# Second attention: four heads to a step, the router with its weights held, and another order of what fills the steps

## The chip, the core and the metric

One core of a Trainium2 chip runs the whole program. TensorE (PE; its weight loads are PEld) multiplies matrices, VectorE (DVE), ScalarE (ACT) and GpSimd (POOL) do the rest, SyncE (SP) issues most transfers. The metric is the device time of one execution in microseconds (us); for the kernel before, the median of three runs. The clock of TensorE can be granted in part; the profile states the granted share as PEclk.

## The reference, cut to what matters

Four sequences of 512 tokens with 512 channels in float32 go through an attention, a feed-forward net with ternary weights, a state-space scan, and a last block of a second attention and a mixture of experts. The change lies in the last block (batch and rows as the kernel has them: 4 x 512):

```python
h = x + attention(rmsnorm(x, ln1_w), ...)      # 16 heads of 32, causal, softmax over 512 keys
out = h + moe(rmsnorm(h, ln2_w), ...)
# moe: a shared expert for all tokens, and the best two of seven routed ones
shared = expert_ffn(x, sh_gate, sh_up, sh_down)
logits = x @ router_w + router_b               # 512 -> 7
probs = sigmoid(logits); scores, idx = top_k(probs, 2)
# expert_ffn: h = silu(x @ wg) * (x @ wu) / 8;  return h @ wd
```

## The kernel before

Inputs stay in SBUF as `xs[b]`, four tiles of 128 tokens x 4 x 512 channels. The stages run one after the other: first attention, ternary net, scan, second attention, experts. The framework that the kernel is written in places the semaphores and orders the instructions of DVE, ACT, POOL and the queues by itself; where `manual_schedule` names PE, PE's instructions keep the order of the code.

**PSUM** in the second attention is cut into two pairs of banks (`pair`, each 2 x 512 floats a partition) and four single banks (`bank`).

**The first attention** (`scores` in `attend`, L318 to L329) computes four heads at a time: 32 rows of channels for each head, so the four matmuls stand on four row quarters of the array and write to two pairs.

**The second attention** works on `pairs`, 128 steps: batch b, group g of four heads, row tile t of 128 queries, and a pair p of heads. A step runs, in this order, `soften` of its own pair (scores into one pair of banks; the mask added on DVE, the maximum on DVE, the exponentials and their sums on ACT), `turn` of the pair two steps back (the probabilities transposed on PE, copied out by DVE for the first head and ACT for the second), every second step `weigh` of a finished row tile (probabilities times values, four heads on four column quarters), and after the last row tile of a group `divide` and `turn_back`. Widths grow with t: 128, 256, 384, 512 columns.

Three generators give a step more work, one piece per `next`:

- `enter(b)`, the way in: layer norm and RMS norm (DVE, ACT, POOL), transposes, the two latents (L715), and for each row tile values, queries, keys and rotation (L734 to L764; the projection holds a pair of banks, `pqd`), then transposes. The first batch's runs before the loop; the next one's begins at step 9 of 32, one piece a step.
- `leave(b)`, the way out: output projection (L984), residual and its write to `acc`, RMS norm, transposes, the write of `hrows`, and the router (L1010: for each row tile the tokens are the weights of the matmul and the 7 columns of `wr` move). It begins at step 6 of the next batch.
- `shared(b)`, the shared expert: transposes, gate and up (L943, one pair of banks `pge` for each half of the inner width, used by gate in one piece and by up in the next), Silu on ACT (L948), down (L957), added to `xs[b]` (L961).

After the loop come the last batch's way out, with `shared(0)` between its output projection and its norm, then the head of the experts' stage, where `shared(1)` and `shared(2)` stand between the small steps of the routing, then 38 tiles of routed tokens, then `shared(3)`, and at the end each of 16 tiles of `acc` is read (L1396), added to `xs` (L1397) and written out (L1398).

Of the kernel before, what the change touches and what calls it, by code (L numbers as in the profile page):

```python
# [45 lines left out]
def block_kernel(ctx: ExitStack, tc: tile.TileContext, a: dict, out: bass.AP):  # L46
# [16 lines left out]
    def pair(name):  # L63
        return banks["pair"].tile([P, 2, 512], F32, tag="pair", name=name)

    def bank(name):
        return banks["bank"].tile([P, 512], F32, tag="bank", name=name)
# [703 lines left out]
    with tc.tile_pool(name="c_f", bufs=2, reuse_waits="tile") as cf, tc.tile_pool(  # L771
# [31 lines left out]
        def turn(b, n, half):  # L803
            bu = [bank("bu") for _ in range(2)]
            for i in range(2):
                k = 2 * half + i
                for t in range(NT):
                    nc.tensor.transpose(  # L808
                        bu[i][:, t * P : (t + 1) * P], scaled[b, n][t][:, k * P : (k + 1) * P], ident
                    )  # L810
            turned[b, n, half] = bu
# [9 lines left out]
        def weigh(b, n, half):  # L821
            if half == 0:
                cb = c1.tile([P, T], F32, tag="cb", name="cb", bufs=3)
                nc.sync.dma_start(cb, c_rows[b, n].partition_broadcast(P))
                weighed[b, n] = cb
            hc = c2.tile([P, 2, T], F32, tag="hc", name="hc", bufs=3)
            nc.gpsimd.tensor_tensor(  # L827
                hc, states.pop((b, n, half)), weighed[b, n].unsqueeze(1).to_broadcast([P, 2, T]), ALU.mult
            )
            states[b, n, half] = hc  # L830
# [93 lines left out]
    def fetch_shared():  # L924

        for tag, name, shape in (
            ("w_a", "sh_gate", [P, NK, INTER]), ("w_b", "sh_up", [P, NK, INTER]), ("w_c", "sh_down", [P, NI, C])
        ):
            sh[name] = dw.tile(shape, F32, tag=tag, name=name)
            nc.sync.dma_start(sh[name], by_rows(a[name]))  # L930
# [35 lines left out]
    with tc.tile_pool(name="d_1", bufs=1) as d1, tc.tile_pool(name="d_2", bufs=2) as d2, tc.tile_pool(  # L966
# [9 lines left out]
        def leave(b, oT):  # L976


            h = hs[b]
            ss = d2.tile([P, NT], F32, tag="ss", name="ss")  # L980
            for t in range(NT):
                y = bank("y")
                for k in range(NK):
                    nc.tensor.matmul(  # L984
                        y, oT[:, k, t * P : (t + 1) * P], wow[:, k, :], start=k == 0, stop=k == NK - 1
                    )
                nc.vector.tensor_tensor(h[:, t, :], h[:, t, :], y, ALU.add)
                n = b * NT + t
                nc.sync.dma_start(acc[n * P : (n + 1) * P, :], h[:, t, :])
                sq = d2.tile([P, C], F32, tag="row", name="sq")  # L990
                nc.scalar.activation(sq, h[:, t, :], AF.Square, accum_out=ss[:, t : t + 1])
                if t == NT - 1:
                    rs = root_inverse(d2, ss, RMS_EPS, 1.0 / C, "rms")
                yield
            hT = far.tile([P, NK, T], F32, tag="hT", name="hTr")
            for t in range(NT + 1):
                if t < NT:
                    nc.vector.scalar_tensor_tensor(
                        h[:, t, :], h[:, t, :], rs[:, t : t + 1], ln2, ALU.mult, ALU.mult
                    )  # L1000
                if t > 0:
                    transpose_into(hT, h[:, t - 1, :], (t - 1) * P)
                if t < NT:
                    yield
            nc.sync.dma_start(by_tokens(hrows, b), h)
            yield
            for t in range(NT):
                pl = bank("plr")
                for k in range(NK):
                    nc.tensor.matmul(  # L1010
                        pl[:, :NR], hT[:, k, t * P : (t + 1) * P], wr[:, k, :],
                        start=k == 0, stop=k == NK - 1,
                    )
                nc.vector.tensor_tensor(logit[:, b * NT + t, :], pl[:, :NR], br, ALU.add)
                if t % 2 == 1:
                    yield

        pairs = [
            (b, g, t, p) for b in range(B) for g in range(NG) for t in range(NT) for p in range(HG // 2)
        ]
        probs, turned_probs, sums, averages, rows, outs = {}, {}, {}, {}, {}, {}

        def soften(b, g, t, p):
            w = (t + 1) * P
            qkT = ready[b][0]
            if (b, g) not in sums:
                sums[b, g] = d2.tile([P, NT, HG], F32, tag="sums", name="sums")  # L1030
            sc = pair("scd")
            for i in range(2):
                at = slice((2 * p + i) * D, (2 * p + i + 1) * D)
                nc.tensor.matmul(  # L1034
                    sc[:, i, :w], qkT[at, g, t * P : w], qkT[at, NG + g, :w], start=True, stop=True
                )
            nc.vector.tensor_tensor(  # L1037
                sc[:, :, t * P : w], sc[:, :, t * P : w],
                neg.unsqueeze(1).to_broadcast([P, 2, P]), ALU.add,
            )  # L1040
            nm = d3.tile([P, 2], F32, tag="nm", name="nm")
            nc.vector.tensor_reduce(nm, sc[:, :, :w], AX.X, ALU.max, negate=True)  # L1042
            pr = d3.tile([P, 2, T], F32, tag="pr", name="pr")
            for i in range(2):
                nc.scalar.activation(  # L1045
                    pr[:, i, :w], sc[:, i, :w], AF.Exp, bias=nm[:, i : i + 1],
                    accum_out=sums[b, g][:, t, 2 * p + i : 2 * p + i + 1],
                )
            probs[b, g, t, p] = pr

        def turn(b, g, t, p):
            w = (t + 1) * P
            pr = probs.pop((b, g, t, p))
            for i in range(2):
                tp = bank("tpd")
                for j in range(t + 1):
                    nc.tensor.transpose(  # L1057
                        tp[:, j * P : (j + 1) * P], pr[:, i, j * P : (j + 1) * P], ident
                    )
                pt = d3.tile([P, T], F32, tag="pt", name="ptd", bufs=7)  # L1060
                if i == 0:
                    nc.vector.tensor_copy(pt[:, :w], tp[:, :w])  # L1062
                else:
                    nc.scalar.copy(pt[:, :w], tp[:, :w])
                turned_probs[b, g, t, 2 * p + i] = pt

        def weigh(b, g, t):
            if t == 0:
# [29 lines left out]
        def turn_back(b, g):  # L1098
            if g == 0:
                outs[b] = d1.tile([P, NK, T], F32, tag="oT", name="oTd")  # L1100
            o = rows.pop((b, g))
            tp = bank("tpb")
            for t in range(NT):
                nc.tensor.transpose(tp[:, t * P : (t + 1) * P], o[:, t, :], ident)
            nc.scalar.copy(outs[b][:, g, :], tp)

        with tc.manual_schedule(engines={mybir.EngineType.PE}):
            for _ in come:
                pass
            left = iter(())  # L1110
            n = len(pairs)
            each = n // B
            for m in range(n + 9):
                b, at = divmod(m, each)
                if m < n:
                    soften(*pairs[m])
                if 2 <= m < n + 2:
                    turn(*pairs[m - 2])
                if m >= 4 and m % 2 == 0 and m - 3 < n:
                    weigh(*pairs[m - 3][:3])  # L1120
                if m >= 6 and m - 6 < n and pairs[m - 6][2:] == (NT - 1, 0):
                    divide(*pairs[m - 6][:2])
                if m >= 8 and m - 8 < n and pairs[m - 8][2:] == (NT - 1, 0):
                    turn_back(*pairs[m - 8][:2])

                if m == (B - 1) * each:
                    fetch_shared()
                if m >= each and at == 6:
                    left = leave(b - 1, outs[b - 1])
                if at >= 7:  # L1130
                    next(left, None)
                if at == 9:
                    come = enter(b + 1, d2) if b + 1 < B else iter(())
                if at >= 9:
                    next(come, None)

            for _ in range(2):
                next(left)
            for _ in shared(0, d1, "lat"):
                pass  # L1140
            for _ in left:
                pass
# [4 lines left out]
    with tc.tile_pool(name="e_1", bufs=1, reuse_waits="tile") as e1, tc.tile_pool(  # L1147
# [7 lines left out]
            nc.sync.dma_start(wgu[:, e, :, INTER:], by_rows(a["r_up"][e]))  # L1155
            nc.sync.dma_start(wdn[:, e], by_rows(a["r_down"][e]))

        second, third = shared(1, e1, "hid"), shared(2, e1, "hid")

        def go(parts, n):  # L1160
            for _ in range(n):
# [226 lines left out]
                turn_hidden(i)  # L1388


        for _ in shared(3, e1, "hid"):
            pass
        for b in range(B):
            for t in range(NT):
                n = b * NT + t
# [64 lines left out]
```

## Time and profile before

| | us |
|---|---|
| median of three runs | 1999.05 |
| the three runs | 1985.09, 1999.05, 2003.15 |
| the profiled execution, its own time | 2001.53 |
| its span, first to last instruction | 1999.8 |
| second attention, first to fourth batch's scores | 1184.1 to 1632 |
| end of the routed tiles on PE, last scatter landed | 1963.1, 1972.1 |

| engine | busy us in the span | share |
|---|---|---|
| PE | 1808.3 | 90% |
| PEld | 1094.2 | 55% |
| DVE | 1152.5 | 58% |
| ACT | 946.8 | 47% |
| POOL | 583.9 | 29% |

The mean granted clock is 0.953. Busy time of PE is that of pipelined instructions whose ends are modelled: a block's cost is better read from its start to the start of the next block. A float32 matmul shows as two instructions. In tables by stretch the columns are the stretch, its length, the busy time and count of each engine, the clock, the DMA engines' share and GB/s. In lists of groups, the line, engine, operation, names and shapes stand ahead of the count; then busy time and mean length in ns, then idle time of the engine before them and what ended it.

### The profile page before, as it was taken

Reading aid. Unit: us, or ns where it says so; the run is one execution under the profiler, and the core shown is the slowest. Engines: PE = TensorE matmul, PEld = TensorE weight load, DVE = VectorE, ACT = ScalarE, POOL = GpSimd, SP = SyncE. Lnnn points to the kernel's source line nnn. Section 1 sums busy time; section 2 is a strip of 40 time slices with the busy share of each in tenths; the row PEclk is TensorE's granted clock in tenths of the full one; section 3 lists DMA queues with packets and bytes.
Section 4 is the critical chain, followed back from the end, with each engine's and each line's share of the span. In section 5 each row is a group of like instructions: output and inputs, shape, how many; then the busy total and the mean of one; then the engine's idle time right before and its main releaser. Section 6 shows DMA issues by size and latency. Waiting matters only on the chain. (4 is left out here: it accounts for less than half of the span.)

```text
span 1999.8 us, 26954 instructions
## 1 busy us (share of the span) xinstructions
PE 1808.3 (90%) x10030; PEld 1094.2 (55%) x10030; DVE 1152.5 (58%) x1908; ACT 946.8 (47%) x1941; POOL 583.9 (29%) x390
## 2 busy tenths in 40 slices
PE   6999899989999897977887789999999998999997
PEld 3434343437766665766776645655565554554553
DVE  5455634376554636999998866655646542422223
ACT  2433353323242426988999846655646542111110
POOL 2221212120202022968998910101001000144431
PEclk9999899999999998979999979989979889999999
DMA  6000230012000104122411100010000105345546
GB/s 240 1 1 1 75 94 1 1 43 74 1 27 17 42 1 142 51 99 82 145 59 48 38 1 1 1 43 1 22 33 22 43 17 177 107 84 94 91 74 189
DMA packets 70629, 114.25 MB, mean 57 GB/s; under 512 B 7962, under 2 KB 26778, under 8 KB 70500
## 3 DMA queue, kind: packets, MB, share of 16 engines
q1 hardware_dynamic: 59268, 86.97, 13.4%
q0 software_dynamic: 8928, 21.37, 5.9%
q10 hardware_dynamic: 2304, 4.20, 0.5%
q8 instruction: 81, 1.33, 0.3%
q14 instruction: 48, 0.39, 0.1%
HBM read 81.18 MB, written 31.33 MB: 56 GB/s over the span
## 5 line engine op out<-in xcount | busy, mean ns | idle before, releaser
L827 POOL TENSOR_TENSOR hc<-h,cb 128x1024 f32<-128x1024 f32 x128 | 304.0, 2418 | 41.8 <-DVE h L816 21.5
L816 DVE TENSOR_TENSOR_SCAN h<-da,bu 128x512 f32<-128x512 f32 x256 | 289.9, 1196 | 14.4 <-ACT da L800 7.6
L808 PE MATMUL bu<-ident,bu 128*128 128x128 f32 x1024 | 166.2, 291 | 53.5 <-DVE h L816 30.5
L249 PE MATMUL pq<-wqkv,hT 128*128 128x512 f32 x384 | 180.1, 617 | 2.8 <-DVE sc_w L173 2.8
L808 PEld LDWEIGHTS bu<-ident,bu 128*128 128x128 f32 x1024 | 122.2, 147 | 87.2 <-ACT bu L794 53.2
L800 ACT ACTIVATE da<-delta_l,am 128x511 f32<-128x511 f32 x256 | 163.9, 709 | 3.8 <-DVE h L816 3.7
L794 ACT ACTIVATE bu<-dxT,bts 128x512 f32<-128x512 f32 x256 | 163.8, 709 | 0.4 <-PE bu L808 0.4
L840 PE MATMUL ys<-ident,hc 128*128 128x128 f32 x1024 | 142.6, 283 | 13.3 <-POOL hc L827 10.5
L1045 ACT ACTIVATE pr<-scd,nm 128x128 f32<-128x128 f32 (+3 forms) x256 | 132.8, 526 | 33.3 <-DVE nm L1042 29.3
L613 PE MATMUL pg<-hTh,w 128*128 128x512 f32 (+1 forms) x352 | 140.5, 399 | 3.2 <-DVE sil L619 2.5
L613 PE MATMUL pg<-hTl,w 128*128 128x512 f32 (+1 forms) x352 | 140.0, 398 | 0.2 <-DVE hTl L603 0.2
L1347 PE MATMUL pgr<-wgu,gTe 128*128 x304 | 137.1, 593 | 0.0
L329 ACT ACTIVATE pt<-sc 128x1024 f32<-128x1024 f32 (+3 forms) x128 | 84.2, 698 | 104.1 <-PE sc L324 102.4
L840 PEld LDWEIGHTS ys<-ident,hc 128*128 128x128 f32 x1024 | 120.6, 147 | 22.6 <-POOL hc L827 18.3
L1034 PE MATMUL scd<-qkTd 32*128 32x512 f32 (+3 forms) x512 | 118.2, 545 | 12.1 <-ACT pr L1045 9.3
L249 PEld LDWEIGHTS pq<-wqkv,hT 128*128 128x128 f32 x384 | 72.0, 196 | 96.2 <-issue 86.0
L1057 PEld LDWEIGHTS tpd<-ident,pr 128*128 128x128 f32 x640 | 75.2, 152 | 68.5 <-issue 36.9
L1057 PE MATMUL tpd<-ident,pr 128*128 128x128 f32 x640 | 109.5, 307 | 1.3 <-DVE ptd L1062 0.8
L101 POOL TENSOR_TENSOR ri_ln<-ri_ln,minus_half 128x4 f32<-128x4 f32 x16 | 16.3, 1018 | 317.1 <-DVE ri_ln L100 317.0
L1042 DVE TENSOR_REDUCE nm<-scd 128x2 f32<-128x256 f32 (+3 forms) x128 | 104.0, 813 | 0.0
L1037 DVE TENSOR_TENSOR scd<-scd,neg 128x256 f32<-128x256 f32 x128 | 54.9, 429 | 82.5 <-PE scd L1034 79.8
L330 POOL TENSOR_SCALAR_AFFINE_SELECT pt<-pt 128x512 f32<-128x512 f32 x64 | 45.1, 704 | 195.2 <-ACT pt L329 195.1
(259 smaller groups left out, 3174.3 us busy)
## 6 DMA issues: line engine op xcount, KB each, us to landing
cb<-c_rows SPq DMA_DIRECT2D x64, 256.0 KB, 3.1
q_w<-in_w2T SPq DMA_DIRECT2D x20, 256.0 KB, 2.5
deltas<-delta SPq DMA_DIRECT2D x16, 256.0 KB, 2.1
dxs<-st SPq DMA_DIRECT2D x16, 256.0 KB, 2.4
delta_l<-deltas SPq DMA_DIRECT2D x4, 1024.0 KB, 9.4
dxT<-dxs SPq DMA_DIRECT2D x4, 1024.0 KB, 7.5
acc<-h SPq DMA_DIRECT2D x16, 256.0 KB, 2.0
hrows<-h SPq DMA_DIRECT2D x4, 1024.0 KB, 4.3
```

The lines of the kernel that those rows point to most:

```text
L249: nc.tensor.matmul(y, inputs_T[b][:, k, t * P : (t + 1) * P], wqkv[:, k, s * C : (s + 1) * C], start=k == 0, stop=k == NK - 1,)
L613: nc.tensor.matmul(pg[:rows, i, :], w[:, k, f * P : f * P + rows], part[:, k, :], start=k + m == 0, stop=k + m == NK,)
L794: nc.scalar.activation(row, dxT[:, t, :], AF.Copy, scale=bts[:, b, t * NS + n : t * NS + n + 1])
L800: nc.scalar.activation(da[:, k, 1:], delta[:, k, 1:], AF.Exp, scale=am[:, k, n : n + 1])
L808: nc.tensor.transpose(bu[i][:, t * P : (t + 1) * P], scaled[b, n][t][:, k * P : (k + 1) * P], ident)
L816: nc.vector.tensor_tensor_scan(h[:, i, :], decays[b, n][:, 2 * half + i, :], bu, 0.0, ALU.mult, ALU.add)
L827: nc.gpsimd.tensor_tensor(hc, states.pop((b, n, half)), weighed[b, n].unsqueeze(1).to_broadcast([P, 2, T]), ALU.mult)
L840: nc.tensor.matmul(sums[b][t][:, k * P : (k + 1) * P], hc[:, i, t * P : (t + 1) * P], ident, is_transpose=True, start=n == 0 and k == 0, s ...
L1034: nc.tensor.matmul(sc[:, i, :w], qkT[at, g, t * P : w], qkT[at, NG + g, :w], start=True, stop=True)
L1045: nc.scalar.activation(pr[:, i, :w], sc[:, i, :w], AF.Exp, bias=nm[:, i : i + 1], accum_out=sums[b, g][:, t, 2 * p + i : 2 * p + i + 1],)
L1057: nc.tensor.transpose(tp[:, j * P : (j + 1) * P], pr[:, i, j * P : (j + 1) * P], ident)
L1347: nc.tensor.matmul(pg, gT[:, k, :], wgu[:, bass.ds(e, 1), k, :].rearrange("p e o -> p (e o)"), start=k == 0, stop=k == NK - 1,)
```

## The change

Five edits, all from the second attention on:

1. `units` take the place of `pairs`: a step is a row tile of all four heads, 64 steps in place of 128. `soften` takes both pairs of banks and puts the four heads on the four row quarters; probabilities are held head by head (7 buffers of 512 in place of 3 of 1024). `turn` is one step behind, `weigh` two, `divide` three, `turn_back` four.
2. The router holds `wr` as weights and moves the 512 tokens: four matmuls, a copy, four small transposes, one addition.
3. `enter` of the next batch begins at step 0 of 16 with a list of pieces for each step; `leave` of the last batch begins at step 3, its router ends in step 0 of the batch after.
4. In the last batch `shared(0)` takes the place of `enter`: its 12 pieces run in steps 0 to 9. The shared weights are fetched in the last step of the third batch.
5. After the loop `shared(1)` stands where `shared(0)` stood; the head of the experts has `shared(2)` and `shared(3)`; none is left after the routed tiles.

```diff
+            pl = bank("plr")
+            for k in range(NK):
+                nc.tensor.matmul(pl[:NR, :], wr[:, k, :], hT[:, k, :], start=k == 0, stop=k == NK - 1)
+            lT = d1.tile([P, T], F32, tag="avs", name="lT")[:NR]
+            nc.scalar.copy(lT, pl[:NR, :])
+            yield
+            tp = bank("tpl")
             for t in range(NT):
-                pl = bank("plr")
-                for k in range(NK):
-                    nc.tensor.matmul(
-                        pl[:, :NR], hT[:, k, t * P : (t + 1) * P], wr[:, k, :],
...
+                nc.tensor.transpose(
+                    tp[:, t * NR : (t + 1) * NR], lT[:, t * P : (t + 1) * P], ident[:NR, :NR]
+                )
...
-            sc = pair("scd")
-            for i in range(2):
-                at = slice((2 * p + i) * D, (2 * p + i + 1) * D)
+            both = [pair("scd") for _ in range(2)]
+            for i in range(HG):
+                at = slice(i * D, (i + 1) * D)
                 nc.tensor.matmul(
-                    sc[:, i, :w], qkT[at, g, t * P : w], qkT[at, NG + g, :w], start=True, stop=True
-                )
...
+                    both[i // 2][:, i % 2, :w], qkT[at, g, t * P : w], qkT[at, NG + g, :w],
+                    start=True, stop=True,
+                )
+            for p, sc in enumerate(both):
...
+                nm = d3.tile([P, 2], F32, tag="nm", name="nm", bufs=4)
+                nc.vector.tensor_reduce(nm, sc[:, :, :w], AX.X, ALU.max, negate=True)
+                for i in range(2):
+                    pr = probs[b, g, t, 2 * p + i] = d3.tile([P, T], F32, tag="pr", name="pr", bufs=7)
...
-            for m in range(n + 9):
+            for m in range(n + 4):
                 b, at = divmod(m, each)
                 if m < n:
-                    soften(*pairs[m])
+                    soften(*units[m])
                 if 2 <= m < n + 2:
-                    turn(*pairs[m - 2])
...
+                    weigh(*units[m - 2])
+                if 1 <= m < n + 1:
+                    turn(*units[m - 1])
+                if 3 <= m < n + 3 and units[m - 3][2] == NT - 1:
+                    divide(*units[m - 3][:2])
+                if 4 <= m and units[m - 4][2] == NT - 1:
+                    turn_back(*units[m - 4][:2])
...
+                if m < n:
+                    if at == 0:
+                        come = enter(b + 1, d2) if b + 1 < B else shared(0, d1, "lat")
+                    pace = (2, 2, 2, 2, 3, 2, 1, 1, 1, 1, 1, 1, 1, 0, 0, 0) if b + 1 < B else (2, 2) + 8 * (1,) + 6 * (0,)
+                    for _ in range(pace[at]):
+                        next(come, None)
+                    if at == each - 1 and b + 1 == B - 1:
+                        fetch_shared()
+                if at == 3 and b > 0:
                     left = leave(b - 1, outs[b - 1])
-                if at >= 7:
-                    next(left, None)
-                if at == 9:
-                    come = enter(b + 1, d2) if b + 1 < B else iter(())
-                if at >= 9:
-                    next(come, None)
-
-            for _ in range(2):
+                if b < B or at == 0:
+                    for _ in range((1, 0, 0, 1, 1, 1, 0, 0, 0, 0, 0, 1, 2, 2, 1, 1)[at]):
+                        next(left, None)
+
+            for _ in range(NT):
                 next(left)
-            for _ in shared(0, d1, "lat"):
+            for _ in shared(1, d1, "lat"):
                 pass
...
-        second, third = shared(1, e1, "hid"), shared(2, e1, "hid")
+        second, third = shared(2, e1, "hid"), shared(3, e1, "hid")
...
-        for _ in shared(3, e1, "hid"):
-            pass
         for b in range(B):
```

## What I expected before the run

> **What bounds the kernel now.** I read the page first (span and slices), then a table of the four batches of the second attention, then TensorE's instructions in order of time, then the groups by form.
>
> ```profile
> span 1999.8 us, 26954 instructions
> ...
> PE   6999899989999897977887789999999998999997
> ...
> PEclk9999899999999998979999979989979889999999
> ```
>
> A slice is 50 us. The second attention fills slices 24 to 33: PE is busy nearly all the time, yet the granted clock is not full. Its four batches:
>
> ```profile
> core 0: us, PE busy (x) PEld busy (x) DVE busy (x) ACT busy (x) POOL busy (x), PEclk, DMA share, GB/s
> 1184.10:1284.90 100.80, 95.40 (x681) 56.64 (x680) 58.21 (x134) 60.28 (x187) 5.10 (x4) 0.88 0.00 1
> 1284.90:1404.00 119.10, 114.79 (x840) 69.67 (x840) 69.02 (x159) 70.69 (x215) 7.13 (x6) 0.96 0.05 19
> 1404.00:1531.70 127.70, 122.86 (x840) 75.08 (x840) 69.25 (x159) 70.80 (x215) 7.13 (x6) 0.89 0.09 30
> 1531.70:1632.00 100.30, 96.42 (x756) 57.18 (x756) 62.47 (x132) 58.76 (x186) 1.02 (x1) 0.86 0.06 22
> ```
>
> Together 447.9 us. PE sets the pace; DVE and ACT have about half the time free. The second and third batch run the same instructions, and one takes 8.6 us more at a lower clock.
>
> ```profile
> 1454.90:1458.30 3.40, 2.63 (x40) 2.27 (x40) 3.26 (x7) 1.46 (x5) 0.00 (x0) 1.00 0.01 4
> 1458.30:1485.60 27.30, 27.30 (x149) 18.56 (x148) 12.27 (x29) 11.16 (x36) 0.00 (x0) 0.50 0.00 1
> 1588.00:1615.30 27.30, 27.30 (x160) 15.85 (x159) 12.82 (x28) 12.55 (x41) 0.00 (x0) 0.50 0.00 1
> 930.00:1078.00 148.00, 123.31 (x950) 103.13 (x948) 138.76 (x129) 147.62 (x246) 138.50 (x60) 1.00 0.30 93
> 1980.00:1992.00 12.00, 9.75 (x18) 3.86 (x19) 6.26 (x10) 0.60 (x1) 0.00 (x0) 0.86 1.05 405
> ```
>
> Twice the clock stands at 0.50 for 27.3 us. The instructions in order of time (start, length, what) tell what ran as it fell, and what a block of scores costs:
>
> ```profile
> 132.43 1.14 PE L324 MATMUL sc<-qkT 32*128 32x512 f32 x8
> 133.50 3.70 PE L249 MATMUL pq<-wqkv,hT 128*128 128x512 f32 x8
> ...
> 1457.05 2.46 PE L1010 MATMUL plr<-wr,hTr 128*128 128x7 f32 x16
> ...
> 1546.74 1.13 PE L1034 MATMUL scd<-qkTd 32*128 32x512 f32 x4
> 1547.80 0.87 PE L1057 MATMUL tpd<-ident,pr 128*128 128x128 f32 x6
> ```
>
> The router (L1010, 7 columns a matmul) runs just before the drop at 1458.3, and again at 1583.7 to 1589.4, around the drop at 1588.0.
>
> **Scores.** In the second attention two heads of 512 columns hold PE from 1546.74 to 1547.80, 1.06 us. In the first attention, which already uses four row quarters, four heads hold it from 132.43 to 133.50, 1.07 us. So four heads cost what two cost. Read in the same way, start of a block to start of the next, two heads take 0.42, 0.63, 0.85, 1.06 us at 128 to 512 columns (sum 2.96; four heads of the first attention 0.43, 0.64, 0.86, 1.07). Per group g of four units t=0 to 3, PE before: scores 2x2.96=5.92, turns 2x(0.37+0.59+0.81+1.02)=5.58, weighing 0.36+0.58+0.79+1.01=2.74, the two transposes of the division 1.1: 15.3 us. After: scores 2.96, turns 4.75 (one change of mode instead of two), the rest the same: 11.5. Over 16 groups PE is relieved of 60 us.
>
> **Fill.** Way in per batch 28.6 us of PE: latents 6.96, four rows of 3.97, transposes the rest. Way out 20: four rows of 3.5, transposes 2.1, router 4.4 (17.7 for four batches), and after the change four matmuls of 512 columns, two instructions of 0.43 each, =3.4 and four small transposes, at most 0.11 each: at most 0.6 us saved, or lost, a batch. Shared expert 22.6: gate and up 13.7, down 6.9, transposes 1.9. The four batches need 74.6, 94.5, 94.5 and 88.9=352.5 us of PE, the last now with shared(0); before, without it, 393.
>
> **The new wait.** Before, a step took one pair of banks and the other was still being read. Now a unit takes both, so the next unit's scores wait until its maximum and exponentials are done, and behind them in PE's order stand weighing, turning and all fill.
>
> ```profile
> L1037 DVE TENSOR_TENSOR scd<-scd,neg 128x256 f32<-128x256 f32 x128 | 54.9, 429 | 82.5 <-PE scd L1034 79.8
> ...
> L1042 DVE TENSOR_REDUCE nm<-scd 128x2 f32<-128x1024 f32 x24 | 29.1, 1213 | 0.0
> L1045 ACT ACTIVATE pr<-scd,nm 128x512 f32<-128x512 f32 x48 | 32.6, 686 | 8.6 <-DVE nm L1042 8.5
> ...
> L948 ACT ACT_TABLE_LOAD  x2: 1283/1283/1283, 1654.1 to 1685.1; - x2
> ```
>
> No unit of before shows this wait, so I bound it. Upper end, nothing overlaps: scores, then two masks (0.43) and two reductions (0.41, 0.68, 0.95, 1.21), two last exponentials (0.36, 0.47, 0.58, 0.68) and 0.65 us between engines (0.2, 0.35, 0.1 read off the steps): 3.5, 4.4, 5.4, 6.4 us for t=0 to 3. Lower end, the pairs slide apart and DVE's own work is the limit (masks, reductions, two copies, the division): 3.1, 2.8, 4.7, 4.4. I take the middle, 3.3, 3.6, 5.0, 5.4, or 17.3 a group: a group without fill takes 17.1 us now (1284.9 to 1302.0). For each of the 64 steps I take the larger of this wait and PE's work, adding in steps 0 to 5 of the first three batches the way in's DVE work (two bn_stats with aggregation 1.7; norms 1.4; rows at 0.75), which now stands in the wait. Sums by batch: 96, 105, 105, 94=400 us; lower end 388, upper end 418.
>
> On top: in steps 7 to 10 the way in's projections hold one of the two pairs; the second half of the scores waits for rotation and copies of their last part, 0 to 1.5 us, I take 0.5, 12 times: 6. In the last batch the shared expert's gate runs in step 2 and its up in step 3 out of one pair of banks, while step 3's scores need both, and again in 4 and 5; and Silu among exponentials loads tables four times at 1.28 (before, the two loads stood outside the attention). From 0 (all under PE's work) to 13 (two waits of 4, 5.1 of loads); I take 7. The first outputs (L984) now follow the transpose they read in the same step: its copy (0.58) has 2.6 us of other rows to hide under; uncovered it would cost 1 us three times.
>
> **Clock.** The router's replacement streams 512 columns a matmul, so I count both 27.3 us stretches as gone. That is already in the sums, which are at full clock. Left: the slow start, which the attention inherits from the head (1184.1 to 1223.1 has a mean clock of 0.68), and new short ones where PE idles in steps without fill. 0 to 20 us; I take 8.
>
> The skill speaks against this: "TensorE: Matmul & The Clock Gate", Part 4, says that transposes do not count as a busy TensorE. By it about 28 steps without fill, mostly transposes, would stay at half clock, an estimate of 5.8 us a group or 40 in all, and the time some 2012. This trace disagrees: from 930 to 1078 PE ran the scan's transposes at 1.00. And "TensorEngine Tiling (Array Packing)", Performance Considerations, warns that after such tiling PSUM's readers can become the bottleneck; by it my upper end, 418, would hold.
>
> **Tail.** shared(3) leaves the end, 22.6 us of PE. But the last scatter lands at 1972.1, and until 1992 the DMA engines are full (share 1.05, 405 GB/s) with reading acc and writing out, 8.4 MB. Only what comes after, the last additions and writes from about 1994, moves up: 1 to 4 us, I take 2.5. The head keeps its length: shared(1) stands where shared(0) stood, and (2), (3) where (1), (2) stood.
>
> **Queues.** SP now gets the shared weights behind hrows (4.3 us) at the end of the third batch; the first is needed two steps, about 8 us, later: nothing, or 2 us if late. POOL is nearly idle there. The router's row buffer was last read a step earlier: nothing.
>
> **Sum.** 400+6+7+8=421 against 447.9: -27. Tail -2.5. From the profiled execution's own 2001.5 us (span 1999.8), 1972. The median shown is 2.5 below it and the three runs spread over 18 us, so I leave it at 1972. Lower end 388 and a tail of -4: 1938; all upper ends, 418+18+13+20=469, and a tail of -1: 2022.
>
> **Rivals.** (1) Nothing gained, about 2000: shared(0) is not absorbed. The last batch takes its 100.3 plus 22.6 instead of 94 to 101, some 25 us more, while the 22.6 taken from the tail were hidden under DMA anyway. For: shared(0) and the way out meet in steps 3 to 5 (10 us a step) while later steps are nearly empty. Against: PE's sum there is 88.9. (2) Slower, 2030: the wait takes the place of PE's work and starves it, and the clock halves. At the upper end a group without fill takes 19.7; at half clock PE alone needs 23, and scores inside the wait double: 26. Seven such groups cost 9 more each than my 17.3, 61 us, and -29.5 turns to +30. It decides once such a group takes over 22 us, since then the relief is used up. For: PE is left with 11.5 of 17.3 us, and old stretches with little in the array did drop the clock. Against: dense fill follows within a few steps and ended such stretches (1485.6, after the latents began). (3) Better, 1938: the pairs slide freely; DVE is at only 58 to 69 us a batch.
>
> **How the numbers follow.** Forecast 0.47, (1) 0.26, (2) 0.14, (3) 0.13. Faster by over 1% (20 us, about what this kernel's measurement can tell): forecast and (3), 0.60; within 1%, (1), 0.26; slower, 0.14. The forecast's own range is 1950 to 1990; with (1) and most of (3) 1942 to 2010.
>
> **What would show it.** L1034 with four heads in one block, 8 instructions, at 1.07 us; no 27 us at 0.50 beside L1010's successor; groups without fill at 16 to 19 us; batches of 96, 105, 105, 94 plus waits; ACT_TABLE_LOAD four times in the last batch; after the scatter still some 25 us to the end. I am wrong if PE waits for ACT's pr before every score block for more than 2 us, or if the clock is below 0.85 in the attention.

## The result, and the profile after

The changed kernel takes 2098.2 us (median of four runs, 2094.8 to 2103.7) beside 2001.1 for the kernel before on the same chip: ratio 1.050, 95% interval 1.046 to 1.054. It is slower by 97 us where 27 less was forecast. Its page, span and slices:

```profile
span 2093.1 us, 26819 instructions
...
PE   6999899989989998778878888878877878999993
...
PEclk9999899999999999989999789989999999999997
```

The slices of the second attention (now the 23rd to 34th) have 7 and 8 where before (24th to 33rd) they had 8 once and then 9. PE has less to do (1788.1 us busy, 1808.3 before) in a longer span. By stage, in us: the loop from the first scores to the first row of the last way out 541.6 (453.0 before), from there to the routed tiles 107.4 (104.9), tiles 220.8 (220.6), and after the last matmul of the tiles 35.0 (37.3). Nearly all of the loss is in the loop. The first scores also start 4.3 us later than before; that start lies between 1181.9 and 1189.9 in the runs below, so I read nothing into it. The table of its four batches, columns as before:

```profile
1188.40:1305.80 117.40, 96.79 (x683) 60.41 (x682) 61.39 (x136) 62.74 (x196) 6.12 (x5) 0.84 0.00 1
1305.80:1445.80 140.00, 113.53 (x821) 67.61 (x820) 70.43 (x155) 71.28 (x218) 7.13 (x6) 0.93 0.04 16
1445.80:1588.60 142.80, 115.58 (x825) 68.34 (x824) 70.25 (x154) 68.50 (x207) 6.14 (x5) 0.92 0.09 27
1588.60:1730.00 141.40, 113.10 (x849) 62.75 (x850) 67.60 (x139) 65.88 (x195) 1.01 (x1) 0.90 0.04 16
```

DVE and ACT (third and fourth pair of numbers) have about the same busy time as before. PE is idle some 20 to 28 us a batch, where before it was idle 4 to 5. The list of waits, PE in the loop (total us, times, longest), says for what:

```profile
PE scd L1040 <- DVE qkd L760: 24.5, 12, 2.4
PE tpd L1064 <- ACT ptd L1071: 23.3, 18, 2.3
PE tpd L1064 <- DVE ptd L1069: 19.5, 25, 1.4
PE scd L1040 <- ACT pr L1053: 11.1, 4, 4.7
```

Two waits are new in this size: scores wait for the rotation of the way in's projections (2.8 us in all before), and the turn waits for its own copies. The wait of scores for exponentials was there before (9.3 us, 19 times, at most 2.1); now it comes four times and is up to 4.7 long. These four make 78 of the 103 us in which PE stands idle. Before, the turn hardly waited, as the idle time at the end of its group's line in the page says (before, then after):

```profile
L1057 PE MATMUL tpd<-ident,pr 128*128 128x128 f32 x640 | 109.5, 307 | 1.3 <-DVE ptd L1062 0.8
```

```profile
L1064 PE MATMUL tpd<-ident,pr 128*128 128x128 f32 x640 | 113.0, 317 | 46.1 <-ACT ptd L1071 23.3
```

**Wait one, the turn.** PE's instructions in one step of the second batch, in order of time (start, length, what, idle before):

```profile
1336.39 0.71 PE L1040 MATMUL scd<-qkTd 32*128 32x256 f32 x8
1337.03 1.08 PE L1082 MATMUL avd<-ptd,vd 128*32 128x128 f32 x32
1338.05 0.55 PE L1064 MATMUL tpd<-ident,pr 128*128 128x128 f32 x3
1340.01 0.33 PE L1064 MATMUL tpd<-ident,pr 128*128 128x128 f32 x1 [1.42 <-ACT avs L1088]
1340.18 1.09 PE L127 MATMUL tp<-ident,row_d 128*128 128x128 f32 x8
1341.11 3.60 PE L984 MATMUL y<-wow,oTd 128*128 128x512 f32 x8
1344.64 0.60 PE L1040 MATMUL scd<-qkTd 32*128 32x384 f32 x4
```

Four heads' scores are one block of 8 instructions, as forecast (0.64 us at 256 columns from start to next start). Three heads are turned, then PE stands still for a bank: four singles exist and the weighing of the group just ended holds one until ACT has copied it. The fill (L127, L984) stands behind the turn in PE's order, so it can't use the gap. All engines in the like step without fill show why copies come late:

```profile
1293.01 0.69 DVE L1050 TENSOR_REDUCE nm<-scd 128x2 f32<-128x512 f32 x1
...
1293.40 0.55 PE L1064 MATMUL tpd<-ident,pr 128*128 128x128 f32 x3
1293.62 0.42 DVE L1045 TENSOR_TENSOR scd<-scd,neg 128x256 f32<-128x256 f32 x1
1293.80 0.47 ACT L1053 ACTIVATE pr<-scd,nm 128x256 f32<-128x256 f32 x1 [1.30 <-PE tpd L1064]
1294.08 0.69 DVE L1050 TENSOR_REDUCE nm<-scd 128x2 f32<-128x512 f32 x1
...
1294.69 0.48 DVE L1069 COPY ptd<-tpd 128x128 f32<-128x128 f32 x2
```

Three turned tiles are there by 1293.95. DVE first does mask and maximum of heads 2 and 3, and copies only from 1294.69; ACT is at the exponentials.

**Wait two, the projections.** The same view where the way in projects queries and keys into one of the two pairs:

```profile
1376.09 1.89 PE L741 MATMUL pqd<-wrk,hTd 128*128 128x256 f32 x8
...
1377.91 0.70 PE L1040 MATMUL scd<-qkTd 32*128 32x256 f32 x4
1378.08 0.37 ACT L749 COPY qkd<-pqd 128x256 f32<-128x256 f32 x1 [2.49 <-PE pqd L741]
1378.55 0.49 DVE L754 TENSOR_TENSOR rotd<-pqd,sin 128x128 f32<-128x128 f32 x2 [4.76 <-ACT qkd L749]
...
1379.40 0.37 ACT L749 COPY qkd<-pqd 128x256 f32<-128x256 f32 x1 [0.95 <-DVE qkd L760]
...
1380.77 0.70 PE L1040 MATMUL scd<-qkTd 32*128 32x256 f32 x4 [2.16 <-DVE qkd L760]
```

Scores of heads 0 and 1 start at 1377.91, those of 2 and 3 at 1380.77, when copy, rotation, copy, rotation have run one after the other. This happens 12 times.

**A wait that the list hides.** The list counts idle PE only, and the modelled end of a matmul can cover a short wait. The weight loads (PEld) show it, here in a unit of 384 columns without fill:

```profile
1295.28 0.30 PEld L1040 LDWEIGHTS scd<-qkTd 32*128 32x128 f32 x4
1296.27 0.30 PEld L1040 LDWEIGHTS scd<-qkTd 32*128 32x128 f32 x4 [0.69 <-ACT pr L1053]
```

Heads 2 and 3 start 0.99 us after heads 0 and 1, once the last exponentials of the unit before have given the second pair free. In 28 of the 64 units the second two heads come late like this, 12 times behind the rotation and 16 times behind exponentials. From the start of the scores to the next instruction, all units together, PE spends 112 us; the count of the forecast was 47 (16 x 2.96), and two heads a step take 100 in e1.

**Wait three, the shared expert.** PE in the last batch:

```profile
1605.67 2.31 PE L943 MATMUL pge<-hTe,sh_gate 128*128 128x512 f32 x5
1607.91 1.13 PE L1040 MATMUL scd<-qkTd 32*128 32x512 f32 x4
1613.71 2.08 PE L1040 MATMUL scd<-qkTd 32*128 32x512 f32 x4 [4.67 <-ACT pr L1053]
```

Gate holds a pair from one step into the next, so heads 2 and 3 wait until the exponentials of 0 and 1 give the other one up. On the way to that stand mask, maximum, and one of the four table loads on ACT:

```profile
1610.91 1.28 ACT L1053 ACT_TABLE_LOAD   x1 [2.30 <-DVE nm L1050]
```

**The fill is added whole.** I cut each unit (from its scores to the next unit's) into PE's time in the attention's own lines and in those of the fill, waits counted to the instruction before them. The two parts add up to the time by this way of cutting; what tells something is whether the own part is smaller where there is fill. Four units without fill (the last three of the first batch and the first of the second), then units 4 to 7 and 8 to 11 of the second batch, by window:

```profile
1291.74:1309.46 17.72, 14.72 (x161) 9.18 (x161) 13.61 (x29) 12.28 (x43) 0.00 (x0) 1.00 0.01 2
1327.61:1365.89 38.28, 32.34 (x224) 18.31 (x223) 18.27 (x36) 17.77 (x54) 0.00 (x0) 1.00 0.06 22
1365.89:1419.70 53.81, 40.73 (x236) 24.94 (x235) 20.73 (x53) 20.81 (x58) 5.11 (x4) 0.87 0.00 1
```

The first takes 17.7 and is all own part, the second is 18.0 own + 20.2 fill, the third 29.7 + 24.2. Over the loop the own part is 18.9 us for four units in the 12 units without fill, and 22.0 in the 51 with fill. So fill hides no wait here, and where the projections are it makes the own part longer. With two heads a step (e1) it is the other way round: 17.9 without fill, 15.8 with it. By TensorE's need alone the own part of four heads would be 11.5.

### The profile page after: what moved, and what is told of

It reads as the page before. It is cut to its first block, busy times and chain, and to the rows that moved or that the text cites. A ratio compares the mean times of both kernels' runs of the same rounds, so it can differ in the third digit from the quotient of the medians.

```text
span 2093.1 us, 26819 instructions
## 1 busy us (share of the span) xinstructions
PE 1788.1 (85%) x9950; PEld 1074.9 (51%) x9950; DVE 1156.4 (55%) x1896; ACT 950.4 (45%) x1949; POOL 584.6 (28%) x390
## 5 line engine op out<-in xcount | busy, mean ns | idle before, releaser
L1064 PE MATMUL tpd<-ident,pr 128*128 128x128 f32 x640 | 113.0, 317 | 46.1 <-ACT ptd L1071 23.3
L1064 PEld LDWEIGHTS tpd<-ident,pr 128*128 128x128 f32 x640 | 80.8, 159 | 77.0 <-ACT ptd L1071 29.0
L1040 PE MATMUL scd<-qkTd 32*128 32x512 f32 (+3 forms) x512 | 83.0, 541 | 35.9 <-DVE qkd L760 24.5
L764 POOL TENSOR_TENSOR qkd<-qkd,rotd 128x512 f32<-128x512 f32 x16 | 20.7, 1291 | 306.1 <-DVE qkd L760 306.1
L101 POOL TENSOR_TENSOR ri_ln<-ri_ln,minus_half 128x4 f32<-128x4 f32 x16 | 16.3, 1019 | 317.0 <-DVE ri_ln L100 316.9
```

Source lines behind the costliest of these rows:

```text
L1064: nc.tensor.transpose(tp[:, j * P : (j + 1) * P], pr[:, j * P : (j + 1) * P], ident)
```

## The experiments

Medians; each has 1997 to 2001 us for the kernel before on its chip. *Loop* is from the profile as above. *Own* and *fill* are the two parts, summed over 63 units of the loop; *half* is the time at half clock, in stretches that begin between 1150 and 1760 us.

| run | us | ratio, interval | loop | own | fill | half |
|---|---|---|---|---|---|---|
| before | 1999 | 1 | 453.0 | 282.2 | 157.9 | 95.6 |
| after | 2098.2 | 1.050 (1.046–1.054) | 541.6 | 337.7 | 187.6 | 119.5 |
| e1 router alone | 1979.2 | 0.990 (0.988–0.991) | 428.8 | 262.5 | 153.4 | 37.5 |
| e2 shared back | 2069.8 | 1.035 (1.033–1.037) | 518.8 | 333.2 | 169.2 | 146.8 |
| e3 pqd in banks | 2068.3 | 1.035 (1.033–1.038) | 520.6 | 314.0 | 190.2 | 92.2 |
| e4 turn spread | 2074.5 | 1.037 (1.035–1.039) | 529.6 | 331.6 | 181.8 | 102.4 |
| e5 new places, two heads | 2030.5 | 1.017 (1.014–1.020) | 481.4 | 278.2 | 187.5 | 68.3 |
| e6 four heads, old places | 2041.9 | 1.023 (1.020–1.026) | 487.7 | 314.7 | 159.3 | 92.2 |
| e7 three undone | 2036.2 | 1.020 (1.018–1.023) | 486.6 | 306.3 | 163.7 | 95.6 |
| e8 fill first | 2029.5 | 1.015 (1.013–1.018) | 479.7 | 287.5 | 172.7 | 95.6 |
| e9 one bank | 2077.7 | 1.038 (1.035–1.041) | 532.9 | 323.7 | 192.8 | 133.1 |
| e10 fill first, one bank | 2030.6 | 1.015 (1.012–1.018) | 479.3 | 283.5 | 176.2 | 119.5 |
| e11 router, one bank | 1985.5 | 0.993 (0.991–0.996) | 434.0 | 266.5 | 153.1 | 30.7 |
| e12 mask left out | 2080.4 | 1.041 (1.038–1.045) | 532.1 | 327.3 | 188.9 | 122.9 |
| e13 old places, relieved | 2005.3 | 1.004 (1.003–1.006) | 454.5 | 278.6 | 163.2 | 61.4 |
| e14 mask on PE | 2045.1 | 1.025 (1.021–1.029) | 486.1 | 316.4 | 154.6 | 27.3 |

**My theory** after seeing the profile: a unit that takes both pairs and turns four tiles at once runs out of PSUM, and the fill, which takes pairs and banks too, adds to it. **Rivals**: the clock; the new places of the fill; DVE's and ACT's chain; the router.

### e1: the router alone

Before, with only the four matmuls of 512 columns, copy and small transposes in place of `plr`'s old loop (edit 2).

> The kernel before with one edit: the router holds its weights and moves 512 tokens. Theory (the loss after sits in the filled steps of the attention, not in the router): this edit alone is no loss; the two stretches of 27.3 us at half clock inside the attention go, the attention shortens by 10 to 27 us, time 1972 to 1990 against about 2000. Rival (the router's extra copy, transposes and waits in the middle of the steps are a part of the loss): slower than before by 5 us or more. Second rival (the clock falls anyway, for the weak load of the steps and not for the router): the long stretches are replaced by others of the same sum, time within 5 us of before.

Measured 1979.2. The batches of this run:

```profile
1185.10:1285.90 100.80, 95.40 (x681) 56.65 (x680) 58.22 (x134) 60.27 (x187) 5.10 (x4) 0.88 0.00 1
1285.90:1403.60 117.70, 113.36 (x820) 66.04 (x820) 68.58 (x156) 70.97 (x216) 7.13 (x6) 0.97 0.05 19
1403.60:1518.90 115.30, 110.49 (x820) 64.23 (x820) 68.22 (x156) 70.80 (x216) 7.13 (x6) 1.00 0.10 33
1518.90:1613.90 95.00, 88.33 (x781) 50.33 (x782) 63.30 (x135) 60.11 (x189) 1.02 (x1) 1.00 0.06 23
```

The third batch, 127.7 at a clock of 0.89 before, takes 115.3 at 1.00. Both long stretches at half clock beside the old router are gone, and nothing came in their place; the first of the three routers in the old loop (1340.3 to 1345.4) had only 3.4 us of half clock behind it. The loop is 24 us shorter. Of the parts tried this is the only one that pays, and it gives the fastest kernel here, by 1%.

### e2, e3, e4: one wait taken away at a time

From the changed kernel. e2:

```diff
-                        come = enter(b + 1, d2) if b + 1 < B else shared(0, d1, "lat")
+                        come = enter(b + 1, d2) if b + 1 < B else iter(())
```
and `shared` (0) after the loop, (1), (2) in the head, (3) after the tiles. e3:

```diff
-                pq = pair("pqd")
+                pq = [bank("pqd") for _ in range(2)]
```
e4:

```diff
+                if 1 <= m < n + 1:
+                    turn(*units[m - 1], (0, 1))
                 if 2 <= m < n + 2:
                     weigh(*units[m - 2])
                 if 1 <= m < n + 1:
-                    turn(*units[m - 1])
+                    turn(*units[m - 1], (2, 3))
```

> The changed kernel with the shared experts where they stood before: shared(0) after the loop, (1) and (2) in the head, (3) after the routed tiles; the last batch has only the way out as fill. Theory (a piece of gate or up holds one of the two pairs over a step, and Silu loads tables in among the exponentials): the last batch goes from about 130 us to 98 to 105, 22.6 us of TensorE work stays after the loop as in both kernels, the tail is 2.4 longer: 2068 to 2078 against 2098. Rival (shared(0) fills idle steps at no cost, the last batch is long for the four heads alone): the loop shortens by under 5 us, time 2095 to 2103.

> The changed kernel with the projections of queries and keys in two single banks in place of one of the two pairs, so the scores of heads 2 and 3 no longer wait for the rotation. Theory (the held pair is a main term: 12 gaps of 2.3 to 2.6 us before L1040 and the late softmax behind each): 29 us go at once, and up to as much again behind them: 2045 to 2070 against 2098; in steps 7 to 10 of the first three batches the waits of scd for qkd are gone. Rival (single banks are the scarce thing: the turn takes four, the weighing holds one): the gaps only move to the transposes of the turn, time 2085 to 2115.

> The changed kernel with the turn of four heads cut in two, heads 0 and 1 ahead of the weighing and heads 2 and 3 behind it, so two copies out of the banks can run under the weighing. Theory (the burst of four tiles finds too few free banks; the trace of after has 43 us of waits of tpd for its own copies): 15 to 35 us less, 2063 to 2083 against 2098, with the waits of tpd for ptd at half or less. Rival (the copies are late because ACT and DVE are still at the exponentials and maxima, wherever the turn stands): the waits keep their sum, time 2093 to 2103.

Measured 28, 30 and 24 us less, each in the range of its theory, e3 at its upper end. In e2 the last batch goes from 141.4 to 109.1 (98 to 105 expected): the 22.6 us of `shared(0)` had cost 32. The loop of that profile is only 23 shorter, since its other batches take 2 to 5 us more each, with 27 us more at half clock. Of e3 and e4, PE's waits in the loop:

```profile
PE tpd L1064 <- ACT ptd L1071: 29.2, 20, 2.4
PE tpd L1064 <- DVE ptd L1069: 28.0, 31, 1.5
PE scd L1040 <- ACT pr L1053: 11.1, 4, 4.7
```

```profile
PE scd L1040 <- DVE qkd L760: 24.5, 12, 2.4
PE tpd L1064 <- DVE ptd L1069: 16.3, 29, 1.3
PE scd L1040 <- ACT pr L1053: 16.1, 12, 4.7
```

In e3 the wait for `qkd` is gone, and the turn's waits have grown from 43 to 57: part of the rival is true, the projections now take the turn's banks. In e4 the turn's waits fall from 43 to 18, ACT's copies from 23.3 to 1.9 and DVE's from 19.5 to 16.3; the scores' wait for `pr` has grown by 5.

### e5 and e6: heads against places

e5 is before with the new router and every new place of the fill, its pieces dealt over the two steps of a unit. e6 is the changed kernel with the old places:

```diff
-                    pace = (2, 2, 2, 2, 3, 2, 1, 1, 1, 1, 1, 1, 1, 0, 0, 0) if b + 1 < B else (2, 2) + 8 * (1,) + 6 * (0,)
...
+                    if at == 4:
+                        come = enter(b + 1, d2) if b + 1 < B else iter(())
+                    for _ in range(0 if at < 4 else 1 if at == 4 else 2):
+                        next(come, None)
```

> Two heads a step as before, with everything else of the change: the new router, the way in from the first step, the way out by the new list, shared(0) in the last batch, (1) after the loop, (2) and (3) in the head. Each unit's pieces are dealt over its two steps. Theory (what makes the fill dear is that a unit of four heads takes both pairs and turns four tiles at once): the fill costs its TensorE time and little more. From 1979 with the router alone, shared(0) adds its 22.6 us to a stage that TensorE bounds, and the tail gives 2.4 back: 1990 to 2010. Rival (the new places of the fill are the fault: DVE's norms ahead of the maxima, and the way out meeting the shared expert in the last batch): 2050 or more, whatever the number of heads.

> Four heads a step and the new router, with the fill where it stood before: the way out from step 3, the way in from step 4, two pieces a step, shared experts at their old places. Theory (four heads make the fill dear): steps with projections, two of them in one step, hold both pairs, and the turn bursts: 2030 to 2065, over the 1979 of the router alone, in spite of the 60 us less of TensorE work. Rival (the new placement is the fault): the forecast's relief shows, 1930 to 1975.

| router new in all | old places | new places |
|---|---|---|
| two heads | 1979.2 | 2030.5 |
| four heads | 2041.9 | 2098.2 |

The new places cost 51 with two heads and 56 with four; four heads cost 63 and 68. The two add up. e6 lies in the range of its theory. My theory missed e5 by 20 us: it lies between theory and rival, so the places are a fault of their own. Its last batch takes 128.3 against 95.0 in e1: 33 for the 22.6 us of `shared(0)` and the new places of the way out, while the tail gives 3.5 back. The second and third batch take 9 and 10 more each, with the same fill.

### e7 to e10: does it add up, and does the order of the step matter

e7 joins e2, e3 and e4. e8 is e7 with the fill behind the scores:

```diff
                     soften(*units[m])
+                if m < n:
+                    ...
+                    for _ in range((2, 2, 2, 2, 3, 2, 1, 1, 1, 1, 1, 1, 1, 0, 0, 0)[at]):
+                        next(come, None)
```
e9 is the changed kernel with one bank for two heads in the turn of 128 and 256 columns, e10 joins e8 and e9:

```diff
-            for i in range(HG):
-                pr = probs.pop((b, g, t, i))
+            per = 2 if 2 * w <= T else 1
+            for i in range(0, HG, per):
                 tp = bank("tpd")
+                for r in range(per):
+                    pr = probs.pop((b, g, t, i + r))
```

> The changed kernel with the three edits that each gave something alone: shared experts at their old places (-28), projections in single banks (-30), the turn cut in two (-24). Theory (three separate waits): the gains add up, 2098 - 82 = 2016, 2006 to 2026. Rival (one idle time seen from three sides, a wait taken away only uncovers the next): 2035 to 2055. Second rival (the granted clock is behind it and comes back once enough waits are gone): 2000 or less, with under 60 us at half clock in the attention.

> The kernel with the three edits undone (2036), and besides it the fill (way in, way out) moved from behind the turn to right behind the scores, ahead of turn and weighing; the way out starts one step later for it. Theory (the waits stand inside the turn, ahead of the fill: its banks wait for copies that DVE and ACT do after the maxima and exponentials of the unit just scored, and the fill comes too late in TensorE's order to cover them): TensorE does the fill while the softmax runs, the copies then find free engines; some 35 filled steps lose 1.3 to 2 us each: 1970 to 1992. Rival (DVE's and ACT's work for a unit sets the pace wherever the fill stands): 2028 to 2044. Second rival (the way in's own copies and norms now stand ahead of the turn's copies in the same queues, and the wait only grows): 2045 or more.

> The changed kernel with one edit: for 128 and 256 columns (half of the units) the turn puts two heads into one single bank and copies both at once, two banks and two copies a unit in place of four. TensorE's work is the same. Theory (the turn's burst on the four single banks is a main term): in those units the wait of 0.8 to 1.7 us inside the turn goes, 32 units: 2055 to 2075 against 2098. Rival (the copies wait for the exponentials anyway): 2090 to 2100.

> Both edits together, fill first and two heads to a bank of the turn, on the kernel with the three edits undone. Theory: 1950 to 1980, under the router alone (1979), for now the 60 us less of TensorE work for the scores can show. Rival (the unit of four heads is bound by its chain of mask, maximum and exponentials over both pairs): 1985 to 2030.

The three gains add to 82 alone and give 62 together: as the first rival had it, what is taken away partly uncovers the next. e8 gives only 7 where my theory had 44 to 66, and e10 nothing beyond it. e8 lies in the range of its first rival, DVE's and ACT's work for a unit, and e10 just above the range of its own, the chain over both pairs: that the waits hurt because they stand ahead of the fill is at most a small part of the cause. The own part falls by 19 us, but the fill's part grows by 9, for PE now waits elsewhere (e8, PE's waits in the loop):

```profile
PE tpd L1064 <- DVE ptd L1069: 11.4, 18, 1.4
PE scd L1040 <- ACT pr L1053: 11.3, 17, 2.1
PE tpd L1064 <- ACT qkTd L128: 8.0, 3, 2.8
PE tpd L1064 <- ACT hTr L128: 6.7, 4, 2.1
```

The turn's tiles now wait for copies of the fill's tiles (`qkTd`, `hTr`): the same four banks, asked for by others. e9 gives 20 in the median, just short of its theory, and 9 in the profiled loop (own part 14 less, fill 5 more); with the turn cut in two already (e10) the same edit gives none. Both edits relieve one scarcity.

### e11: one bank a pair with two heads

Before with the new router and the turn of e9.

> Two heads a step and the old fill as before, with the new router and the turn of 128 and 256 columns put into one bank for the two heads of a step, one copy in place of two. Theory (with two heads a step TensorE bounds, its waits for copies are small): 1970 to 1982, no clear gain over the 1979 of the router alone. Rival (copies and banks hold up the steps here too): 1950 to 1968.

Measured 1985.5, 6 us over e1 and 3 over the theory's range: with two heads there are no banks to gain.

### e12 to e14: DVE's chain or the banks

e12 takes the `nc.vector.tensor_tensor` of the mask out of the changed kernel, so it leaves out the causal mask within a row's own tile and is of use for its time alone. e13 is e6 with e3, e4 and e9. e14 is e13 with the mask on TensorE:

```diff
+            for i in range(HG):
+                nc.tensor.matmul(
+                    both[i // 2][:, i % 2, t * P : w], ident, neg, start=False, stop=True, skip_group_check=True
+                )
```

> The changed kernel with the addition of the mask left out (128 instructions of DVE at 0.43 us, 55 us in all; the softmax then covers the later keys of a row's own tile as well). TensorE's work, banks and fill are the same. Theory (a unit waits for the chain that frees its pairs and the turn's banks, and DVE is in it: mask and maximum of both pairs, then the copies): 0.4 to 0.9 us of every unit, 25 to 55 us less, 2043 to 2073 against 2098. Rival (banks and TensorE's order alone, DVE has half its time free): under 10 us less, 2088 or more.

> Four heads with the router and the fill at its old places (2042), and with three reliefs of the banks: projections in single banks, the turn cut in two, two heads to a bank for 128 and 256 columns. Theory (PSUM waits are most of the 63 us that four heads cost there): 1985 to 2015. Rival (DVE's and ACT's chain on both pairs costs it): 2025 to 2042.

> The kernel with the three reliefs and the mask moved from DVE to TensorE, which adds a matmul of the mask's 128 columns to each head's scores: 55 us less of DVE, some 55 us more of TensorE (256 matmuls of two instructions at 0.11). Theory (TensorE has 11.5 of 18 us to do in a unit's group and DVE's chain is what it waits for): faster than without this edit by 10 to 30 us in spite of the added TensorE work. Rival (TensorE and banks bound): slower by 20 to 55 us.

e12 gives 18 in the median (10 in the profiled loop) of the 55 us that DVE no longer works: between the two expectations, so DVE's chain is in it, at a third of its size or less. It shows in the units without fill, where the own part of four units falls from 18.9 to 16.4 us; in those with fill it hardly moves (22.0 to 21.8). e13 gives 37 of the 63 that four heads cost, without a change to DVE's work on the scores: banks are the larger part. Its gain lies in the units with fill (own part 20.6 us a group in e6, 16.4 in e13); without fill nothing is gained (19.1 and 19.6). The largest waits left there, PE in the loop:

```profile
PE scd L1040 <- ACT pr L1053: 17.4, 26, 2.1
PE tp L127 <- DVE ptd L1071: 7.3, 8, 1.8
```

In e14 that wait for `pr` falls to 2.7, yet the run is 40 us slower, 32 in the profiled loop. What the mask costs on PE stands between the second and third start here:

```profile
1293.97 0.71 PE L1040 MATMUL scd<-qkTd 32*128 32x256 f32 x8
1294.61 1.16 PE L1045 MATMUL scd<-neg,ident 128*128 128x128 f32 x8
1295.61 0.38 PE L1066 MATMUL tpd<-ident,pr 128*128 128x128 f32 x2
```

That is 1.0 us a unit, 64 in all (my estimate was 55). So 24 to 32 us came back elsewhere: from DVE's shorter chain, from the clock (27.3 us at half clock, the least of all, against 61.4) or from both; the run doesn't part them. It shows that the mask doesn't pay on TensorE, not that DVE's chain costs nothing.

## Why the prediction was wrong

**Right:** four heads in one block at the price of two, where both pairs are free (36 units of 64); the long half-clock stretches were the router's (e1); four ACT_TABLE_LOADs in the last batch; the tail (2.5 less, measured 2.3); a group without fill at 16 to 19 us (17.7).

**The step that failed** is "for each of the 64 steps I take the larger of this wait and PE's work". It gave 96, 105, 105, 94; measured 117.4, 140.0, 142.8, 141.4. In this term I priced one wait, for the pairs, and put it behind the fill, where fill would cover it. Without fill it came out as priced: 17.7 us a group, 17.3 taken. But the waits stand at three other points, inside the turn, between heads 1 and 2 of the scores, and within the fill, and the largest are for PSUM. Time is therefore own part plus fill, not the larger of them: the own part is 22.0 us a group with fill, against 11.5 of TensorE's work. So the 60 us of relief never showed. From e1 to the changed kernel PE's time from the start of scores to the next instruction goes from 100 to 112, that of the turn from 97 to 161, where I had counted 47 (16 x 2.96) and 76 (16 x 4.75). With two heads the own part in filled units is 15.8 a group (e1), and TensorE's need is 15.3: there PE's own work fills the time in which a unit of four heads waits. I counted engines and left out the four single banks, which no term of the sum named.

**Terms mis-sized:** the held pair, 0.5 x 12 = 6: copy, rotation, copy, rotation run one after the other, PE waits 2.0 us each time (24.5 in all), and e3 gives 30 with what follows it. The shared expert, 22.6 taken into the room and 7 on top: 32 in e2, so nothing of it was absorbed (33 in e5, with the way out moved as well); this is my first rival, which stood at 25. The turn's burst was not in the sum: 24 (e4). The clock, 8: from e1 to the changed kernel there are 82 us more at half clock, in some twenty stretches of 3.4 to 10.2 us. At half speed that is at most 41 us of loss. How much of it is the clock's own no run settles, but it is not the main cause: the profiled run of e2 is 19 us shorter than that of the changed kernel with 27 us more at half clock, and that of e7 59 us shorter with only 24 less.

**The rival that came nearest** was the slower one, for the wrong place. It looked for starved groups without fill above 22 us and a clock below 0.85; the one group without fill at full clock took 17.7. The mean clock of the attention was 0.90, and below 0.85 only in the first batch (0.84; 0.88 before). The loss sits in the steps with fill, which I had named as the protection.

**A warning set aside.** I left the warning of the Trainium skill's "TensorEngine Tiling (Array Packing)", Performance Considerations, at a bound of 418. That page also says, under Restrictions and Gotchas, that row tiles raise the pressure on PSUM, as different row tiles write to different banks. This case agrees: 24.5 us of waits for a pair that the projections hold, and second heads that come late in 28 units; the 43 us of waits for turned tiles are PSUM too, though no row tiles. The Trainium skill's "TensorE: Matmul & The Clock Gate", Part 1, tells of a kernel whose clock swings because PE idles briefly between groups while cycling through PSUM; the some twenty short stretches at half clock agree with it.

**Open:** e13 has the banks relieved and is still 26 us over e1. By the cut of the loop 11 of these stand in the own part of units without fill (19.6 us a group, 17.9 in e1), 5 in the own part of filled units (16.4 against 15.8), and 10 in the fill. The largest wait left that I found is for the second pair: in 30 units heads 2 and 3 start 0.5 to 1.9 us late, each time behind the exponentials of the unit before, 32 us in all. What a shorter chain on DVE and ACT would give there wasn't tried. Why the fill from step 0 costs 9 to 10 us a batch even with two heads (e5) wasn't taken apart either.

## What to carry to other kernels

When PE has less to do, ask what it will wait for, and count PSUM buffers as you count an engine: who holds each bank, from which matmul to which copy, and in which queue that copy stands. In an order written out by hand, a wait can be covered only by work that stands ahead of it, and work that needs the same buffers covers little (e8: 7 us). Idle time of an engine with modelled ends doesn't show every wait: compare a block's time from start to start with its price. A change of several parts is best taken singly: the router alone, 1979 us (ratio 0.990), beats both kernels, and the other edits bury it.

## What the runs showed that I had not expected

- Filling an attention that already fills PE costs more than the fill: 32 us for 22.6 us of matmuls with four heads (e2), and 33 with two, where the way out moved too (e5).
- The old router's matmuls of 7 moving columns, 96 instructions in the loop, had cost about 24 us of it, mostly through the clock (58 us less at half clock without them); the same work with 512 columns freed it (third batch 0.89 to 1.00).
- Less time at half clock does not mean a shorter time: the profiled run of e2 has 27 us more of it than that of the changed kernel and is 19 shorter; e14 has 27 us of it and takes 2045, with 64 us more work on PE, e13 has 61 and takes 2005.
